# Mask products of two early batches behind a score seed, and half of the value block copies on GpSimd

## The chip, the cores and the metric

The kernel runs on one core of a Trainium2 chip. The metric is the device time of one execution in microseconds (us). The time before is the median of three runs, 596.37 us; the profile is one further execution.

## What is computed

The reference is a graph attention layer on 16 batches of 512 nodes with 512 features, in float32. It adds two directions of attention (d = 0, 1); each node attends with 16 heads of width 32 to the first 20 nodes of its batch. Cut to what matters:

```python
q_exp = where(row_zero, 0, q)                       # row_zero: the node's features sum to 0
self_feat = concat([v, q_exp]) @ W_self.T + b_self  # 512 nodes x 512
output = self_feat
for d in range(2):
    A = (adj if d == 0 else swap(adj))[:, :, :20, :]  # 11 integer labels for each pair of nodes
    cond, vb = A.sum(-1), A @ w_bias + b_bias
    qh, kh = heads(self_feat @ Wq[d].T + bq[d]), heads(self_feat[:, :20] @ Wk[d].T + bk[d])
    aff = where(cond > 0, qh @ kh / sqrt(32), -9e15) + vb
    output += heads_out(softmax(aff) @ self_feat[:, :20], Wout[d]) + bout[d]
return v + relu(output)
```

## The kernel before

**Setup.** The first 100 us or so load the weights and form, for all batches at once, the keys (written to the DRAM tensors `g1_d`, for batch 1, and `g_d`, for the later ones; batch 0's stay in `g0`) and the values (`vw_d`). The values are also needed as small 32x32 blocks with zeros around them: `clear_blocks` fills the DRAM tensor `bd_d` with zeros, and twelve DRAM-to-DRAM copies, `fill_block` 0 to 11 (L185, steps `bl00` to `bl11`), put pieces of 128 bytes from `vw_d` into it. Each copies 64 x r pieces, with r rows from 4 to 20. All batches' blocks are filled by these twelve copies, so the load of batch 0's blocks (`load_values`, step `Lvd`, tile `vd`, four loads a batch) waits for all of them.

**Loop.** After that the work is a list of small steps, each recorded on one engine. `ORDER` (L17) is a table of step names with an offset: in turn t the step `mul3+1` is done for batch t+1. The turns run from -1 to 17, and the code walks through the table once per turn (L1131); a step is left out where `first` (L1108) says that it has no work for that batch. Each engine executes its own steps strictly in this order. Loads are DMAs issued by the sync engine's queue (SP), also in order; `behind` ties a load to an instruction recorded five steps earlier, so that loads don't run ahead. Each DMA also waits until the DMA eight places ahead of it on its queue has landed.

In turn t, TensorE (PE) does three things for 512 nodes: seven score products S1 to S7 of batch t (L440; a fast 2x2 block scheme, accumulated in the PSUM tiles `ps_a` and `ps_d`), the attention sum O of the batch before (L550, which reads `vd`), and seven feature products F1 to F7 of batch t+1 (L292, into four banks `ps_o`). The order on PE is S1, S2, S6, O, S7, S5, F1, S4, F6, S3, F7, F5, F2, F4, F3. Around them stand, by batch t:

- S1 adds to `ps_a`; step `t11` (`take`, L487, ScalarE = ACT) copies it to the softmax tile `s_11`; S6 then adds on to `ps_a`, so it can't start before that copy.
- S2 adds to `ps_d`; `f11` (`join`, L496, VectorE = DVE) adds it to `s_11`. Then `sc` (`seed`, L482, ACT) puts a new start value into `ps_d` for S5.
- `t12` (L492, DVE) takes `ps_a` after S6, and S7 waits for it.
- `mx11` (L503, DVE), `sub11` (L507, GpSimd = POOL), `exp11` (L511, ACT), `sum11` (L515, DVE) and so on are the softmax of `s_11`.
- `z`, `y` and `t` tiles (L409, L421, L267, POOL) are the operand sums of the block schemes.
- `p1` (L337, ACT) copies bank 0 after F1, and F6 reuses the bank.

The masks of batch t+1 are made in turn t too: `load_adj` brings the tile `adj` (a single buffer, two loads), eleven steps `mul0` to `mul10` (`mask_mul`, L363, ACT) multiply one label each by its weight into `prod`, `cnt` (`mask_count`, L369, DVE) sums the labels, `flg` (L375, L376, ACT) turns the sum into a flag, and `msum` (L381, DVE) adds `prod` up. In the table most of the `mul` steps stand ahead of `t11` and `sc`.

Of the kernel before, what the change touches and what calls it, by code (L numbers as in the profile page):

```python
# [17 lines left out]
Z3+0 Z2+0 mul1+1 S2+0 mul2+1 Lx2+1 LG3+1 rec12-1 n22b-2 mul0+1 turn22-1 rb3-2 m22a-1 mul7+1 fu22+0  # L18
turn21-1 bl06+0 nor12-1 bl00+0 bl05+0 t11+0 S6+0 rb1-2 f11+0 bl02+0 P1+0 Lx3+1 Y3+0 u22a-1 turn12-1 e11+0
t12+0 mul9+1 bl09+0 mul10+1 bl11+0 so2-1 mul3+1 P4b-1 mul4+1 Lxn1+2 x22a-1 O0-1 Oa-1 mul6+1 O1-1 Lnz+1  # L20
k1+0 Z1+0 mul8+1 Lxn3+2 S7+0 Y4+0 mul5+1 sc+0 rb2-2 m22b-1 mx11+0 Ladj0+2 kv+1 oe2-1 flg+1 Lvd0+0 k2+0
oe3-1 rs0+2 S5+0 X1+1 sub11+0 LG1+1 oe0-1 F1+1 exp11+0 u22b-1 LG2+1 Lcq+2 ra0-2 v22a-2 rs2+2 t22+0 oe1-1
s22a-1 S4+0 bl01+1 msum+1 rs1+2 Z4+0 bl07+1 sum11+0 LG0+2 f22+0 Lx0+2 v22b-2 bl08+1 sA1-2 rs3+2 mx22+0
X2+1 f21+0 x22b-1 rm+2 p1+1 sp1+1 rec11+0 rb0-2 Ob-2 F6+1 bl04+1 bl10+1 nq+1 rst+2 P3+0 st1-1 ra3-1 bl03+1
nc+1 ra1-1 X3+1 Lxn0+3 sp0+1 S3+0 p2+1 P2+0 Ladj1+2 e21+0 mx21+0 sub22+0 exp22+0 Lvd3+0 nor11+0 nd+1 Oc-2
sub21+0 F7+1 rc0-2 exp21+0 X4+1 Lvd2+0 k3b+0 Lvd1+0 r22a-1 Lxn2+3 f12+0 F5+1 e12+0 sum22+0 p3+1 n22a-1
F2+1 F4+1 sd+1 st3-1 sA0-2 mx12+0 rec22+0 sum21+0 j3+1 sub12+0 rc2-2 nr+1 k0+1 st2-1 rec21+0 k3a+0 F3+1
# [8 lines left out]
def gat_kernel(  # L36
# [20 lines left out]
    nc = tc.nc  # L57
    B, F, N = xT.shape
# [112 lines left out]
    def blocks():  # L171

        bb = bd_d.rearrange("c b r e i g -> (c b) r e i g")
        vv = vw_d.rearrange("d c (b m) (e g) -> d (c b) m e g", m=NG, e=HL)
        for e in range(HL):
            for i in range(2):
                j = (e * S) // 32 + i
                for d in range(2):
                    lo = max(e * S + d * NG, 32 * j)
                    hi = min(e * S + (d + 1) * NG, 32 * j + 32)  # L180
                    if lo < hi:
                        m, r = lo - e * S - d * NG, lo - 32 * j
                        yield bb[:, r : r + hi - lo, e, i], vv[d, :, m : m + hi - lo, e]

    def fill_block(n):  # L185
        to, of = list(blocks())[n]
        nc.sync.dma_start(to, of)

    def ran(ins):
        done["all"].append(ins)  # L190
# [847 lines left out]
    with tc.manual_schedule():  # L1038
# [19 lines left out]
        for n in range(len(list(blocks()))):  # L1058
            steps[f"bl{n:02d}"] = lambda b, n=n: fill_block(n)
# [67 lines left out]
        NOT_END |= {f"{x}22" for x in ("mx", "sub", "exp", "sum", "rec", "nor", "turn")} | {"sa", "sd", "sc", "O0", "O1"}  # L1127
        NOT_END |= {f"{x}{ij}" for x in "tf" for ij in (11, 12, 21, 22)} | {f"{x}{c}" for x in ("oe", "st") for c in range(C)}
        order = [(w[:-2], int(w[-2:])) for w in ORDER.split()]
        fresh = True  # L1130
        turns = [(name, turn_ + ahead) for turn_ in range(-1, B + 2) for name, ahead in order]  # L1131
        for name, b in turns:
            if b in first(name):
                if fresh and (name in ("S6", "nd", "nc") or name[0] == "F" or name[:2] == "so"):
                    fresh = False
# [57 lines left out]
```

## Time and profile before

| what | value |
|---|---|
| runs | 594.38, 596.37, 598.05 us (median 596.37) |
| profiled execution | 591.75 us, its span 590.0 us |
| PE busy | 560.5 us, 95% of the span, 13980 matmuls |
| DVE, ACT, POOL busy | 433.7, 413.4, 427.8 us |
| DMA queue of SP (q1) | 123.73 MB; GpSimd's (q0) 1.36 MB |
| granted TensorE clock | 0.987 over the span |

Busy is the time in which an engine executes something. Since PE is busy for 95% of the span, the question of any change is whether it takes away some of the 29 us in which PE is idle, or adds to them. In the table of forty slices the first slices, up to about 145 us, are where PE, DVE, ACT and POOL are visibly emptier than later.

### The profile page before, as it was taken

Reading aid. Unit: us, or ns where it says so; the run is one execution under the profiler, and the core shown is the slowest. Engines: PE = TensorE matmul, PEld = TensorE weight load, DVE = VectorE, ACT = ScalarE, POOL = GpSimd, SP = SyncE. Lnnn points to the kernel's source line nnn. Section 1 sums busy time; section 2 is a strip of 40 time slices with the busy share of each in tenths; the row PEclk is TensorE's granted clock in tenths of the full one; section 3 lists DMA queues with packets and bytes.
Section 4 is the critical chain, followed back from the end, with each engine's and each line's share of the span. In section 5 each row is a group of like instructions: output and inputs, shape, how many; then the busy total and the mean of one; then the engine's idle time right before and its main releaser. Section 6 shows DMA issues by size and latency. Waiting matters only on the chain.

```text
span 590.0 us, 31439 instructions
## 1 busy us (share of the span) xinstructions
PE 560.5 (95%) x13980; PEld 437.4 (74%) x13980; DVE 433.7 (74%) x628; ACT 413.4 (70%) x890; POOL 427.8 (73%) x374
## 2 busy tenths in 40 slices
PE   8999999697999999998999999999999999999994
PEld 5443356586878787887888888877887777899983
DVE  0576571575878787877888787878787878788765
ACT  1344571786787878786878787878786868786622
POOL 2637945476687878786888887878787878888643
PEclk9999999898999999999999999999999999999997
DMA  8999999878766767766667776767666767652222
GB/s 292 380 396 370 322 316 373 222 180 239 190 222 180 222 192 227 199 209 159 228 196 223 195 222 192 220 172 228 188 215 183 219 185 212 202 175 87 70 93 73
DMA packets 102199, 127.88 MB, mean 217 GB/s; under 512 B 21457, under 2 KB 66545, under 8 KB 100017
## 3 DMA queue, kind: packets, MB, share of 16 engines
q1 hardware_dynamic: 100272, 123.73, 67.5%
q8 instruction: 110, 1.80, 1.3%
q0 software_dynamic: 672, 1.36, 1.0%
q10 hardware_dynamic: 1120, 0.79, 0.4%
q14 instruction: 25, 0.20, 0.1%
HBM read 85.97 MB, written 40.24 MB: 214 GB/s over the span
## 4 chain that ended last, share of the span: by engine, by line
PE 83%; POOL 5%; DMA 4%; issue 4%; DVE 2%; SPq 1%; ACT 1%; DVEq 0%; POOLq 0%; ACTq 0%
PE ps_o L292 30%; PE ps_a L440 22%; PE ps_d L440 15%; PE ps_o L550 8%; PE ps_k L798 3%; PE ps_a L456 1%; DMA ws_q<-in_wsT 1%; DMA vw_d<-v 1%; POOL st L924 1%; POOL cq_d L861 1%; SPq L148 1%; PE ps_kv L748 1%; DMA g_d<-st 1%; PE ps_d L456 1%; DMA xn<-in_xn 1%
## 5 line engine op out<-in xcount | busy, mean ns | idle before, releaser
L507 POOL TENSOR_TENSOR s<-s,top 128x640 f32<-128x640 f32 x63 | 80.5, 1277 | 68.8 <-DVE top L503 68.8
L363 ACT ACTIVATE prod<-adj,wb_sb 128x160 f32<-128x160 int32 x165 | 84.8, 590 | 13.3 <-POOL t L267 7.9
L522 POOL TENSOR_TENSOR s<-s,sum 128x640 f32<-128x640 f32 x63 | 79.8, 1278 | 12.3 <-DVE sum L518 12.1
L440 PE MATMUL ps_a<-y,z 128*32 128x152 f32 x1920 | 74.0, 301 | 13.1 <-issue 8.2
L292 PE MATMUL ps_o<-t,ws_s 128*32 128x246 f32 x1440 | 83.7, 370 | 0.0
L440 PEld LDWEIGHTS ps_a<-y,z 128*32 128x32 f32 x1920 | 64.1, 112 | 21.7 <-issue 18.7
L440 PE MATMUL ps_d<-g,z 128*32 128x152 f32 x1920 | 71.3, 293 | 0.3 <-issue 0.3
L511 ACT ACTIVATE s<-s 128x640 f32<-128x640 f32 x63 | 46.1, 732 | 36.1 <-POOL s L507 35.7
L292 PEld LDWEIGHTS ps_o<-t,ws_s 128*32 128x32 f32 x1440 | 56.0, 110 | 16.6
L440 PEld LDWEIGHTS ps_d<-g,z 128*32 128x32 f32 x1920 | 64.8, 110 | 2.8 <-issue 1.2
L292 PE MATMUL ps_o<-x,ws_v 128*32 128x246 f32 (+1 forms) x960 | 59.4, 373 | 0.3 <-issue 0.3
L560 DVE SCALAR_TENSOR_TENSOR o<-ps_o,x 128x512 f32<-128x512 f32 x60 | 38.4, 683 | 22.9 <-ACT cond L375 9.3
L492 DVE TENSOR_TENSOR s<-ps_a,both 128x640 f32<-128x640 f32 x45 | 37.1, 825 | 23.4 <-PE ps_a L440 23.1
L550 PE MATMUL ps_o<-wt,vd 32*32 32x256 f32 (+1 forms) x2176 | 49.3, 381 | 4.5 <-issue 2.6
L503 DVE TENSOR_REDUCE top<-s 128x32 f32<-128x640 f32 x63 | 51.2, 812 | 0.6
L515 DVE TENSOR_REDUCE sum<-s 128x32 f32<-128x640 f32 x63 | 50.2, 798 | 0.3 <-ACT s L511 0.3
L529 DVE STREAM_TRANSPOSE wt<-s 128x640 f32<-128x640 f32 x63 | 49.4, 802 | 0.0
L533 ACT COPY ps_o<-sf 128x512 f32<-128x512 f32 x64 | 36.6, 587 | 17.7 <-DVE sf L335 15.5
L292 PEld LDWEIGHTS ps_o<-x,ws_v 128*32 128x32 f32 x960 | 37.3, 110 | 13.3 <-issue 0.8
L550 PEld LDWEIGHTS ps_o<-wt,vd 32*32 32x32 f32 x2176 | 30.9, 105 | 19.3 <-issue 6.8
L496 DVE TENSOR_TENSOR s<-ps_d,s 128x640 f32<-128x640 f32 x45 | 36.9, 820 | 9.8 <-PE ps_d L440 9.2
L390 ACT COPY both<-add 32x160 f32<-32x160 f32 x128 | 41.1, 321 | 1.7
(283 smaller groups left out, 1228.0 us busy)
## 6 DMA issues: line engine op xcount, KB each, us to landing
g<-g_d SPq DMA_DIRECT2D x60, 304.0 KB, 3.8
g_d<-st SPq DMA_DIRECT2D x16, 1064.0 KB, 7.3
out_T<-o SPq DMA_DIRECT2D x60, 256.0 KB, 4.0
xn<-in_xn SPq DMA_DIRECT2D x56, 256.0 KB, 3.7
x<-in_xT SPq DMA_DIRECT2D x56, 256.0 KB, 3.6
adj<-in_adj SPq DMA_DIRECT2D x32, 440.0 KB, 4.6
vd<-bd_d SPq DMA_DIRECT2D x64, 64.0 KB, 3.4
nz<-nz_d SPq DMA_DIRECT2D x14, 256.0 KB, 3.8
```

The source lines that it names most:

```text
L292: nc.tensor.matmul(to[bass.ts(a, R), i] if wide else to[bass.ts(a, R), i, :, HK:], lhs, mov, start=wide and i == 0, stop=k == 1, skip_grou ...
L363: ran(nc.scalar.activation(new_prod(b)[:, :, l], adjs[b][:, :, l], AF.Identity, scale=wb_sb[:, l : l + 1]))
L390: ran(nc.scalar.copy(adds[b][bass.ts(2 * pg + hp, R), :, 2 * t : 2 * t + 2], add[bass.ts(2 * pg + t, R)]))
L440: nc.tensor.matmul(to[bass.ts(q, R)], rows[:, k, q // 2, bass.ds((2 * t + u) * R, R)], keys[:, k, q % 2], start=False, stop=k == 1, skip_g ...
L503: ran(nc.vector.tensor_reduce(tops[b, ij], flat(soft_tile(b, ij)), AX.X, ALU.max))
L507: ran(engine.tensor_sub(s, s, tops.pop((b, ij)).unsqueeze(2).to_broadcast([P, 4 * 2 * HL, NG])))
L511: ran(nc.scalar.activation(s, s, AF.Exp))
L515: ran(nc.vector.tensor_reduce(tops[b, ij], flat(soft_tile(b, ij)), AX.X, ALU.add))
L522: ran(engine.tensor_mul(s, s, tops.pop((b, ij)).unsqueeze(2).to_broadcast([P, 4 * 2 * HL, NG])))
L529: ran(nc.vector.transpose(wts[b][:, j, i], soft_t.pop((b, ij)).rearrange("p v h m -> p (v h m)")))
L550: nc.tensor.matmul(to, vds[b][r, j, e, i], w[:, :, bass.ts(block, 32)], start=False, stop=i == 1, skip_group_check=True,)
L560: ran(nc.vector.scalar_tensor_tensor(o, banks[q].rearrange("p (j n) -> p j n", j=2), 0.0, of_out(xs[b], hp, pg), ALU.max, ALU.add))
```

## The change

It has two parts. The first holds back the steps `mul0` to `mul10` and `cnt` of batches 1 and 2: they are put behind the step `sc` of batch 0 and of batch 1. From batch 3 on the order is as before.

The second moves six of the twelve block copies (1, 3, 4, 7, 8 and 10) from SP's queue to GpSimd's, and from the end of turn -1 to a place in turn 0, behind `flg`.

```diff
+    LATER = (1, 3, 4, 7, 8, 10)
+
     def fill_block(n):
         to, of = list(blocks())[n]
-        nc.sync.dma_start(to, of)
+        (nc.gpsimd if n in LATER else nc.sync).dma_start(to, of)
...
-        fresh = True
-        turns = [(name, turn_ + ahead) for turn_ in range(-1, B + 2) for name, ahead in order]
+        fresh, turns, held_back = True, [], []
+        for turn_ in range(-1, B + 2):
+            for name, ahead in order:
+                b = turn_ + ahead
+                early = b in (1, 2) and (name[:3] == "mul" or name == "cnt") and ("sc", b - 1) not in turns
+                (held_back if early else turns).append((name, b))
+                if (name, b) in (("sc", 0), ("sc", 1)):
+                    turns, held_back = turns + held_back, []
```

In the table the six entries `bl01+1`, `bl03+1`, `bl04+1`, `bl07+1`, `bl08+1` and `bl10+1` become `+0` entries between `flg+1` and `Lvd0+0`. Line numbers grow by two behind the first edit: L363 is L365 in the changed kernel.

**ACT at the start of turn 0.** Rows of before: the mask products of batch 1 (`prod` from `adj`), `t11` (copy of `ps_a`), `sc` (copy into `ps_d`), then `kv`, the flag, a row sum and `exp11`.

```order
L363 ACTIVATE prod_1275<-adj_1104,wb_sb 128x160 x4
L487 COPY s_11_1316<-ps_a 128x640
L363 ACTIVATE prod_1275<-adj_1104,wb_sb 128x160 x7
L482 COPY ps_d<-cq_904 128x4x160
L347 COPY sf_1410<-kvn 128x16x5
L375 ACTIVATE cond_1234<-cond_1234,marks 128x160 x2
```

The same place in the changed kernel:

```order
L489 COPY s_11_1303<-ps_a 128x640
L484 COPY ps_d<-cq_904 128x4x160
L365 ACTIVATE prod_1388<-adj_1104,wb_sb 128x160 x11
L349 COPY sf_1404<-kvn 128x16x5
L377 ACTIVATE cond_1386<-cond_1386,marks 128x160 x2
```

Four products no longer stand ahead of `t11`, and none ahead of `sc`; the eleven follow in one piece. On DVE `cnt` (the row `cond<-adj`) moves from ahead of `f11` to behind `t12`. In turn 1 both engines change in the same way.

**GpSimd in turn 0.** Rows of before: operand sums `y` and `z` of batch 0, `t_1` of batch 1, then `sub11`.

```order
L404 TENSOR_TENSOR z_1_1367<-sf_909 128x512
L421 TENSOR_TENSOR y_4_1402<-g_83,y_2_1236 128x608
L267 TENSOR_TENSOR t_1_1451<-x_179 128x492
L507 TENSOR_TENSOR s_11_1316<-s_11_1316,top_11_1406 128x640
L409 TENSOR_TENSOR z_4_1516<-sf_909,z_2_1273 128x512
```

The same place in the changed kernel:

```order
L406 TENSOR_TENSOR z_1_1349<-sf_909 128x512
L423 TENSOR_TENSOR y_4_1383<-g_83,y_2_1228 128x608
L189 DMA bd_d<-vw_d 64x12x32
L189 DMA bd_d<-vw_d 64x20x32
L189 DMA bd_d<-vw_d 64x4x32 x2
L189 DMA bd_d<-vw_d 64x20x32
L189 DMA bd_d<-vw_d 64x12x32
L269 TENSOR_TENSOR t_1_1451<-x_179 128x492
L509 TENSOR_TENSOR s_11_1303<-s_11_1303,top_11_1400 128x640
```

The six copies now stand between `y_4` and `t_1`, with `sub11` behind them.

**SP ahead of the first load of blocks.** Rows of before: start terms `cq` of batch 1, the copies, two parts of batch 1's keys (`g`), the first half of batch 2's mask labels (`adj`), the first of the four `vd` loads.

```order
L148 DMA cq_1221<-cq_d 32x320 x4
L187 DMA bd_d<-vw_d 64x12x32
L187 DMA bd_d<-vw_d 64x4x32
L156 DMA g_1214<-g_d 128x4x152
L187 DMA bd_d<-vw_d 64x20x32
L187 DMA bd_d<-vw_d 64x4x32
L187 DMA bd_d<-vw_d 64x12x32
L187 DMA bd_d<-vw_d 64x20x32
L156 DMA g_1214<-g_d 128x4x152
L187 DMA bd_d<-vw_d 64x16x32
```

The same place in the changed kernel:

```order
L148 DMA cq_1221<-cq_d 32x320 x4
L156 DMA g_1214<-g_d 128x4x152 x2
L189 DMA bd_d<-vw_d 64x16x32
L189 DMA bd_d<-vw_d 64x20x32
L189 DMA bd_d<-vw_d 64x16x32
L189 DMA bd_d<-vw_d 64x8x32 x2
L189 DMA bd_d<-vw_d 64x20x32
L141 DMA adj_1402<-in_adj 128x880
L162 DMA vd_1415<-bd_d 32x2x256
```

Six of the twelve copies are gone from SP, all of them ahead of the loads of `adj` and `vd`.

More of the change, by code (lines that the diff above doesn't have):

```diff
@@ L20 @@
 t12+0 mul9+1 bl09+0 mul10+1 bl11+0 so2-1 mul3+1 P4b-1 mul4+1 Lxn1+2 x22a-1 O0-1 Oa-1 mul6+1 O1-1 Lnz+1
[L21 to L24, printed above, removed]
+k1+0 Z1+0 mul8+1 Lxn3+2 S7+0 Y4+0 mul5+1 sc+0 rb2-2 m22b-1 mx11+0 Ladj0+2 kv+1 oe2-1 flg+1 bl01+0 bl03+0
+bl04+0 bl07+0 bl08+0 bl10+0 Lvd0+0 k2+0 oe3-1 rs0+2 S5+0 X1+1 sub11+0 LG1+1 oe0-1 F1+1 exp11+0 u22b-1
+LG2+1 Lcq+2 ra0-2 v22a-2 rs2+2 t22+0 oe1-1 s22a-1 S4+0 msum+1 rs1+2 Z4+0 sum11+0 LG0+2 f22+0 Lx0+2 v22b-2
+sA1-2 rs3+2 mx22+0 X2+1 f21+0 x22b-1 rm+2 p1+1 sp1+1 rec11+0 rb0-2 Ob-2 F6+1 nq+1 rst+2 P3+0 st1-1 ra3-1
 nc+1 ra1-1 X3+1 Lxn0+3 sp0+1 S3+0 p2+1 P2+0 Ladj1+2 e21+0 mx21+0 sub22+0 exp22+0 Lvd3+0 nor11+0 nd+1 Oc-2
```

## The prediction

> **What bounds the kernel now.** I read the chain that ended last first, then its pieces in order of time, then a table by stage.
>
> ```profile
> PE 83%; POOL 5%; DMA 4%; issue 4%; DVE 2%; SPq 1%; ACT 1%; DVEq 0%; POOLq 0%; ACTq 0%
> ...
> 133.87 3.85 DMA xn<-in_xn
> 138.22 1.49 ACT prod L363 x3
> ...
> 197.36 2.07 PE ps_a L440 x64
> ...
> 226.77 2.07 PE ps_a L440 x64
> ```
>
> PE is the bound, so only time in which PE waits can be won. In the chain (start, duration, what) PE is left at 133.87 for a load and then for mask products on ACT, until about 140. The two last lines are S1 of two successive turns: an undisturbed turn lasts 226.77 - 197.36 = 29.41 us. The table by stage (start:end, length, then each engine's busy us, granted clock, DMA share) shows this hole's end and another one:
>
> ```profile
> 105.00:110.00 5.00, 2.25 (x37) 2.04 (x41) 2.81 (x2) 4.90 (x11) 0.00 (x1) 0.72 0.72 260
> ...
> 140.00:145.00 5.00, 4.58 (x104) 3.65 (x109) 3.90 (x6) 5.00 (x12) 4.88 (x4) 0.66 0.75 225
> ```
>
> The granted clock is 0.72 and 0.66 where PE resumes, so part of the price of a wait is paid behind it.
>
> The PE rows of the timeline (start, duration, what, and in brackets the idle time before it) show which products wait:
>
> ```profile
> 97.38 2.25 PE L440 MATMUL ps_a<-g,sf 128*32 128x152 f32 x64
> ...
> 101.63 1.04 PE L1019 MATMUL ps_o<-zero 128*128 128x512 bf16 x4
> 107.75 3.63 PE L440 MATMUL ps_a<-y,z 128*32 128x152 f32 x64 [5.08 <-issue]
> 112.42 2.27 PE L440 MATMUL ps_a<-y,z 128*32 128x152 f32 x64 [1.04 <-DVE s L492]
> ...
> 120.31 1.87 PE L292 MATMUL ps_o<-t,ws_s 128*32 128x246 f32 x32
> ...
> 132.35 2.28 PE L440 MATMUL ps_a<-g,sf 128*32 128x152 f32 x64
> ...
> 140.42 3.50 PE L440 MATMUL ps_a<-y,z 128*32 128x152 f32 x64 [3.73 <-ACT s L487]
> ...
> 166.90 2.25 PE L440 MATMUL ps_a<-g,sf 128*32 128x152 f32 x64
> ```
>
> S6 waits 5.08 us in turn 0 and 3.73 us in turn 1, both times though S1 has long ended, and takes about 3.6 us where S7 at 112.42 takes 2.27 for as many matmuls. The second wait is put down to `t11` (L487); the first only to "issue". ACT's rows explain both:
>
> ```profile
> 105.10 1.97 ACT L363 ACTIVATE prod<-adj,wb_sb 128x160 f32<-128x160 int32 x4 [7.93 <-POOL t L267]
> 106.98 0.67 ACT L487 COPY s<-ps_a 128x640 f32<-128x640 f32 x1
> 107.55 3.40 ACT L363 ACTIVATE prod<-adj,wb_sb 128x160 f32<-128x160 int32 x7
> 110.85 0.69 ACT L482 COPY ps_d<-cq 128x640 f32<-128x640 f32 x1
> 111.48 0.26 ACT L347 COPY sf<-kvn 128x80 f32<-128x80 f32 x1
> ...
> 114.38 0.74 ACT L511 ACTIVATE s<-s 128x640 f32<-128x640 f32 x1 [0.73 <-POOL s L507]
> ...
> 118.51 0.57 ACT L337 COPY sf<-ps_o 128x492 f32<-128x492 f32 x1 [1.55 <-PE ps_o L292]
> ...
> 137.74 1.97 ACT L363 ACTIVATE prod<-adj,wb_sb 128x160 f32<-128x160 int32 x4 [5.42 <-DMA xn<-in_xn]
> ```
>
> `t11` stands behind four mask products, and these wait for `adj`. At 105.10 the bracket names an engine that was done; DVE's `cnt` starts at the same moment and names the load (`105.09` below). `t11` ends at 106.98 + 0.67 = 107.65, and S6 starts 0.10 us later.
>
> **The change, part by part.** *First wait.* S1 ends at 97.38 + 2.25 = 99.63; with no product ahead of it, `t11` would be done by about 100.3, and S6 can follow the bank clearing at 101.63 + 1.04 = 102.67. That is 5.1 us earlier, and S6 then takes 2.27 instead of 3.63 us. PE alone would reach F6 at 102.67 + (120.31 - 107.75) - 1.36 = 113.9. What is late next is ACT: `adj` still lands at about 105.0, and F6 needs `p1` (118.51). From 105.10 to 118.51 two steps leave the path (`t11`: 107.55 - 106.98 = 0.57; `sc`: 111.48 - 110.85 = 0.63), and two idle pieces (0.73 and 1.55) close up: `p1` starts at 118.51 - 3.48 = 115.03 and F6 at about 115.7 instead of 120.31. First term: **4.6 us**, not 6.4; PE waits 1.8 us at F6. The eleven products cost nothing more than before; they are the same instructions.
>
> DVE must keep up:
>
> ```profile
> 105.09 1.99 DVE L369 TENSOR_REDUCE cond<-adj 128x160 f32<-128x1760 int32 x1 [6.79 <-DMA adj<-in_adj]
> ```
>
> `t12` follows S6 (102.67 + 2.27 = 104.9) and would end near 105.8, `cnt` 1.99 later near 107.8, and `mx11` comes next, more than four us ahead of its place before (GpSimd got its result at 113.08, below). So `cnt`, though now between `t12` and `mx11`, delays nothing that ends last.
>
> *GpSimd's six copies.* They come after `y_4`, with `t_1` and `sub11` queued behind them; `exp11` on ACT waits for `sub11`.
>
> ```profile
> 103.78 1.22 POOL L267 TENSOR_TENSOR t<-x 128x492 f32<-128x492 f32 x1
> 113.08 1.27 POOL L507 TENSOR_TENSOR s<-s,top 128x640 f32<-128x640 f32 x1 [8.07 <-DVE top L503]
> ...
> 46.72 0.99 POOL L883 DMA_DIRECT2D vw_d<-v  x1 [1.62 <-DVE v L881]
> ...
> 59.15 0.77 POOL L883 DMA_DIRECT2D vw_d<-v  x1
> ...
> 63.49 2.56 POOL L861 DMA_DIRECT2D cq_d<-c  x4 [0.29 <-POOL c L859]
> ...
> 69.81 1.31 POOL L883 DMA_DIRECT2D vw_d<-v  x2
> ```
>
> The trace has no such copy on GpSimd, but it has GpSimd DMAs of 64 pieces (0.64 us each, 63.49), 256 pieces (0.655, 69.81) and 512 pieces (0.77, 59.15): 0.64 plus 0.29 ns a piece, an estimate from these rows. Two copies each of 256, 768 and 1280 pieces give 2 x (0.66 + 0.84 + 0.99) = 5.0 us. Bounds: 6 x 0.64 = 3.8 us if the pieces cost nothing, and 4608 x 0.99 / 512 = 8.9 us if the longest row (46.72) were all pieces. I take 5.0, since two of the six shapes equal a row. They begin where `t_1` began, at 103.78, and end at 108.8, `t_1` at 110.0, `sub11` at 111.3; ACT wants it at 114.38 - 0.73 - 1.20 = 112.45. The cover is GpSimd's idle 8.07 us, and 1.1 us of it remains: from 6.1 us of copies on each further one costs one; the upper bound costs 2.8.
>
> *Second wait and the loads.* With `t11` free of the products, turn 1 can be an undisturbed turn: 166.90 - 132.35 = 34.55 against 29.41, a second term of **5.1 us** (3.73 of wait, the rest mostly the slow S6). With S1 of turn 1 at 132.35 - 4.6 = 127.75, O wants its `vd` tiles after three products, at 134.0, and ACT's products must start near 134.3, because 10.5 us lie between the first product and the end of `p1` (105.10 to 115.6) and F6 falls at 144.9. Before, these loads came later:
>
> ```profile
> 108.57 2.16 SPq L187 DMA_DIRECT2D bd_d<-vw_d  x2
> ...
> 111.44 2.81 SPq L187 DMA_DIRECT2D bd_d<-vw_d  x4
> ...
> 115.53 6.66 SPq L187 DMA_DIRECT2D bd_d<-vw_d  x6
> ...
> 124.99 0.34 SPq L162 DMA_DIRECT2D vd<-bd_d  x1
> ...
> 132.03 0.38 SPq L141 DMA_DIRECT2D adj<-in_adj  x1
> 132.50 1.32 SPq L162 DMA_DIRECT2D vd<-bd_d  x3
> ...
> DMA to landing us min/median/max: 3.0/5.2/5.4
> ```
>
> The second `adj` half is issued at 132.03, and the products wait until 137.74; the last line (the `vd` loads of this stage) puts the last `vd` at about 138.6. They must come 4.6 us earlier. SP loses the copies at 108.57 and 111.44, 2.16 + 2.81 = 5.0 us of an unbroken queue, so they land near 132.7 and 133.6, just in time.
>
> The Trainium skill, DMA: Bandwidth & Descriptors, section "Issuing engines are not separate DMA queues", says that DMAs of all issuing engines run on the same 16 engines and that issuing from several saves sequencer time alone. By that rule the 5.0 us of issue may be all that SP gains, and the data of the copies still has to be moved; no row here has both queues on this work.
>
> The bytes can get in the way. The xn loads that `rs` (L198, ahead of `exp11`) reads are then in flight:
>
> ```profile
> 99.33 3.11 SPq L135 DMA_DIRECT2D xn<-in_xn  x4
> ...
> DMA to landing us min/median/max: 9.2/9.3/9.6
> ```
>
> The first lands near 99.33 + 9.3 = 108.6, and ACT would read it in the step ahead of `exp11`, at about 111.7 if I give that step 0.7 us before 112.45: 3.1 us of slack. The six later copies on SP (88 rows of 64 pieces) took 124.99 - 115.53 = 9.5 us until all had landed, so the moved ones (72 rows) are worth at most 7.7 us; if all of that went ahead of the load, `rs` would lose 4.5 us. At the least it is nothing, or a little less than nothing, since the copies start earlier. I take 0.7 us for this and for loads that are just late.
>
> *Sum:* 4.6 + 5.1 - 0.7 = **9.0 us** less. Later turns keep their order and only move. The profiled execution is 591.75 us (span 590.0), so it would become 582.7; it lies 4.6 us under the median of the runs. On that median, 596.37, the forecast is **587.4 us**. One per cent of it, about what a measurement can tell, is 6.0 us.
>
> **The rivals.**
>
> *The loads aren't earlier.* If `adj` and `vd` keep landing at 137.7 and 138.6, O starts 4.6 us late and the gain is 4.4: 592.0. For it: the first `vd` load can't be issued until the last copy has landed, and DMA shares near 1 stand in the table. Against it: SP's queue has no gap between 108.57 and 132.03 that is not its own work or that landing.
>
> *The copies crowd out ACT's inputs.* Either xn is 4.5 us late, or the copies hold GpSimd for 8.9 us: the gain falls to about 4.5 to 6.2, some 591.
>
> *GpSimd is held by each copy* (slower). If GpSimd could not go on until a copy has landed, `t_1`, `sub11` and so `exp11`, `p1` and F6 would stand behind six landings. This decides from 6.1 + 9.0 = 15.1 us in all, 2.5 us a copy. The price, from the landings of GpSimd's small DMAs:
>
> ```profile
> DMA to landing us min/median/max: 3.9/4.4/6.4
> ```
>
> 6 x 4.4 = 26.4 us, 11.3 us slower: 607.7. Against it: four DMAs in 2.56 us at 63.49, each issued long before the one ahead had landed.
>
> A milder form of this stands in the Trainium skill, SBUF - State Buffer, section "SBUF: two separate sides": a VectorE copy in a two-port mode locks GpSimd out while it writes descriptors, 3100 ns instead of 620. As an estimate from that page, six copies would take 18.6 us, 3.5 us slower. Here the DMA at 46.72, beside a VectorE copy, took 0.99 against 0.77, and VectorE does reductions and additions from 105 to 109, not copies; so I give it little.
>
> *The first wait is another's.* The profile calls it "issue". If `t11` is not what S6 waits for, only the second term is left: 592. Against it: the 0.10 us between the two.
>
> **How the numbers follow.** Forecast 0.57, loads not earlier 0.16, crowding 0.14, GpSimd held 0.07, first wait another's 0.06. Faster by over 1% holds the forecast and a part of the crowding, 0.66; within 1% is most of the second, third and fifth case, 0.27; slower 0.07. The range runs from 585 (both terms in full, 9.7, and 1.7 of the spread of the runs) to 593 (a gain of 4.4 and 1.0 of spread) and leaves out about 0.15.
>
> **What would show it.** Right: `t11` by 101 and S6 near 102.7; F6 near 115.7 behind `p1`; six GpSimd DMAs of 0.65 to 1.0 us from 103.8; first `vd` issue near 120; S6 of turn 1 straight behind S2; S1 of turn 2 near 158. Wrong: S6 still waiting with `t11` done; GpSimd's DMAs over 1.5 us each; `rs` waiting for xn; O or the products waiting for loads at 134.

## The result, and the profile after

The changed kernel takes 589.18 us (median of four runs, 587.97 to 591.21) against 597.21 us for the kernel before beside it (594.38 to 600.05): ratio 0.988, 95% interval 0.983 to 0.992. A second measurement on other runs (589.91 against 596.00 us) gave 0.990, interval 0.985 to 0.995. So 6 to 8 us are won. My forecast on the median was 587.4 us, in a range of 585 to 593; the sum behind it was 9.0 us. The profiled executions differ by only 3.0 us, 588.76 against 591.75.

Below, "after" is the changed kernel; its lines are the earlier numbers plus 2. First its PE rows (start, duration, what, in brackets the idle time before it and what ended it), to be read beside those of before:

```profile
99.21 2.25 PE L442 MATMUL ps_a<-g,sf 128*32 128x152 f32 x64
...
104.42 0.46 PE L442 MATMUL ps_a<-y,z 128*32 128x152 f32 x7
106.07 2.13 PE L442 MATMUL ps_a<-y,z 128*32 128x152 f32 x57 [1.19 <-issue]
...
117.65 0.41 PE L294 MATMUL ps_o<-t,ws_s 128*32 128x246 f32 x3
...
129.69 0.29 PE L442 MATMUL ps_a<-g,sf 128*32 128x152 f32 x1
...
133.96 2.32 PE L442 MATMUL ps_a<-y,z 128*32 128x152 f32 x61
136.21 0.71 PE L552 MATMUL ps_o<-wt,vd 32*32 32x256 f32 x32
137.60 2.12 PE L552 MATMUL ps_o<-wt,vd 32*32 32x256 f32 x96 [0.68 <-issue]
139.66 1.23 PE L442 MATMUL ps_a<-y,z 128*32 128x152 f32 x31
143.36 1.32 PE L442 MATMUL ps_a<-y,z 128*32 128x152 f32 x33 [2.47 <-issue]
...
146.49 1.87 PE L294 MATMUL ps_o<-x,ws_v 128*32 128x256 f32 x30
148.76 0.37 PE L294 MATMUL ps_o<-x,ws_v 128*32 128x246 f32 x1 [0.40 <-issue]
...
162.99 0.33 PE L442 MATMUL ps_a<-g,sf 128*32 128x152 f32 x3
```

S1 of turn 0 stands 1.83 us later than in before (99.21 against 97.38), in setup code that is the same in both, so only distances between rows are compared. Both old waits ahead of S6 are gone: S6 of turn 1 runs on from S2, and S6 of turn 0 comes at 104.42, as soon as the banks are cleared. Turn 0, from S1 to S1, fell from 34.97 to 30.48 us. Turn 1 fell only from 34.55 to 33.30, where 29.41 was forecast. New in these two turns are breaks in the middle of products, put down to "issue": S6 after 7 matmuls, O after 32 of 128, S7 after 31 of 64. Nothing in the program divides a product at these places, and in before O and S7 of turn 1 ran through:

```profile
143.85 3.17 PE L550 MATMUL ps_o<-wt,vd 32*32 32x256 f32 x128
146.94 2.27 PE L440 MATMUL ps_a<-y,z 128*32 128x152 f32 x64
```

ACT's rows show what the reorder did:

```profile
101.57 0.69 ACT L489 COPY s<-ps_a 128x640 f32<-128x640 f32 x1 [2.57 <-issue]
...
107.16 5.35 ACT L365 ACTIVATE prod<-adj,wb_sb 128x160 f32<-128x160 int32 x11 [1.96 <-DMA adj<-in_adj]
...
116.95 0.55 ACT L339 COPY sf<-ps_o 128x492 f32<-128x492 f32 x1
...
132.23 0.69 ACT L489 COPY s<-ps_a 128x640 f32<-128x640 f32 x1 [2.42 <-PE ps_a L442]
...
135.81 5.38 ACT L365 ACTIVATE prod<-adj,wb_sb 128x160 f32<-128x160 int32 x11
```

`t11` (L489) is ahead of all eleven products in both turns, and the second time the products start without a wait for `adj`. The GpSimd copies and the queue of SP:

```profile
105.60 4.53 POOL L189 DMA_DIRECT2D bd_d<-vw_d  x6
...
111.75 1.28 POOL L509 TENSOR_TENSOR s<-s,top 128x640 f32<-128x640 f32 x1 [0.34 <-DVE top L505]
```

```profile
122.60 0.34 SPq L162 DMA_DIRECT2D vd<-bd_d  x1
...
129.81 0.38 SPq L141 DMA_DIRECT2D adj<-in_adj  x1
```

Six copies hold GpSimd for 4.53 us; the row by line gives shortest, median and longest in ns:

```profile
L189 POOL DMA_DIRECT2D bd_d<-vw_d x6: 647/771/901, 105.6 to 109.4; - x6
```

On SP, the first `vd` load and the second half of `adj` are issued at 122.60 and 129.81 instead of 124.99 and 132.03; less the later setup that is 4.2 and 4.1 us sooner.

### The profile page after: what moved, and what is told of

It is laid out like the page before. It is cut to its first block, busy times and chain, and to the rows that moved or that the text cites. A ratio compares the mean times of both kernels' runs of the same rounds, so it can differ in the third digit from the quotient of the medians.

```text
span 587.0 us, 31440 instructions
## 1 busy us (share of the span) xinstructions
PE 559.7 (95%) x13980; PEld 438.8 (75%) x13980; DVE 434.5 (74%) x628; ACT 413.4 (70%) x890; POOL 432.1 (74%) x380
## 4 chain that ended last, share of the span: by engine, by line
PE 86%; DMA 3%; issue 3%; POOL 2%; ACT 2%; DVE 1%; SPq 1%; DVEq 0%; ACTq 0%; POOLq 0%
PE ps_o L294 30%; PE ps_a L442 22%; PE ps_d L442 16%; PE ps_o L552 8%; PE ps_k L800 3%; DMA g_d<-st 2%; DMA ws_q<-in_wsT 1%; PE ps_a L458 1%; PE ps_v L877 1%; POOL st L926 1%; PE ps_kv L750 1%; PE ps_d L458 1%; ACT st L917 1%; PE ps_sf L232 1%; ACT sf L325 0%
## 5 line engine op out<-in xcount | busy, mean ns | idle before, releaser
L365 ACT ACTIVATE prod<-adj,wb_sb 128x160 f32<-128x160 int32 x165 | 84.5, 593 | 2.0 <-DMA adj<-in_adj 2.0
L294 PE MATMUL ps_o<-t,ws_s 128*32 128x246 f32 x1440 | 85.2, 370 | 0.0
L442 PE MATMUL ps_a<-y,z 128*32 128x152 f32 x1920 | 72.4, 294 | 8.0 <-issue 7.0
L442 PEld LDWEIGHTS ps_a<-y,z 128*32 128x32 f32 x1920 | 62.6, 110 | 16.6 <-issue 13.3
L442 PE MATMUL ps_d<-g,z 128*32 128x152 f32 x1920 | 72.7, 293 | 0.9 <-issue 0.9
L513 ACT ACTIVATE s<-s 128x640 f32<-128x640 f32 x63 | 46.0, 731 | 34.1 <-POOL s L509 33.7
L294 PEld LDWEIGHTS ps_o<-t,ws_s 128*32 128x32 f32 x1440 | 58.0, 110 | 15.2
L294 PE MATMUL ps_o<-x,ws_v 128*32 128x246 f32 (+1 forms) x960 | 60.8, 373 | 0.4 <-issue 0.4
L294 PEld LDWEIGHTS ps_o<-x,ws_v 128*32 128x32 f32 x960 | 38.9, 110 | 12.4 <-issue 1.1
```

Of the source, the lines that this page charges most:

```text
L294: nc.tensor.matmul(to[bass.ts(a, R), i] if wide else to[bass.ts(a, R), i, :, HK:], lhs, mov, start=wide and i == 0, stop=k == 1, skip_grou ...
L365: ran(nc.scalar.activation(new_prod(b)[:, :, l], adjs[b][:, :, l], AF.Identity, scale=wb_sb[:, l : l + 1]))
L442: nc.tensor.matmul(to[bass.ts(q, R)], rows[:, k, q // 2, bass.ds((2 * t + u) * R, R)], keys[:, k, q % 2], start=False, stop=k == 1, skip_g ...
L513: ran(nc.scalar.activation(s, s, AF.Exp))
```

## The experiments

In all of them "fetch" is the theory that the breaks in the trace of after suggest: the waits called issue are PE waiting for its own instructions.

**The reorder alone.** The table and the copies as before, with the rule that holds the steps back.

```diff
-    LATER = (1, 3, 4, 7, 8, 10)
+    LATER = ()          # and ORDER of the kernel before
```

> The reorder alone: the mask products and counts of batches 1 and 2 stand behind sc, all twelve copies stay on SP at their old places. Two terms (my prediction's): the first wait goes (about 4.6 us), but adj's second half and the vd tiles of turn 1 still land near 137.7 and 138.5, so O waits from about 134 to 138.6 and the second term is lost: 4 to 5 us faster than before, O the product that waits. Rival (fetch): PE cannot run turn 1 without a pause, since its instructions then come too late (the waits called issue in the kernel after, 3.5 us in turn 1); a wait at O costs little because those waits vanish beside it: 5 to 8 us faster, and no wait called issue of over 1 us in the 10 us behind O.

Measured: 592.9 us, ratio 0.997 (0.993 to 1.000), 2.1 us won, just at the edge of what can be told from nothing.

```profile
139.22 3.82 PE L552 MATMUL ps_o<-wt,vd 32*32 32x256 f32 x126 [1.42 <-DMA vd<-bd_d]
...
145.31 1.32 PE L442 MATMUL ps_a<-y,z 128*32 128x152 f32 x33 [0.67 <-issue]
```

O waits for `vd`, as the first theory said, and the break in S7 is 0.67 us instead of 2.47, as the second said. Both put the gain too high.

**The copies alone.** After, with nothing held back.

```diff
-                early = b in (1, 2) and (name[:3] == "mul" ...
+                early = b in () and (name[:3] == "mul" ...
```

> The six copies on GpSimd at their new place, the order of products as before. Two terms: the first wait stays as it was (S6 of turn 0 5 us late behind four products). In turn 1 adj's second half lands near 133 to 135, about when S1 ends at 134.6, so that the four products and t11 are late by 0 to 2 us instead of 3.7: 2 to 4 us faster than before. Rival (each half needs the other): t11 behind the products waits all the same, 0 to 1 us faster.

Measured: 594.31 us, ratio 0.996 (0.992 to 1.000), 2.7 us won. The profiled execution, 600.24 us, was the longest of its runs; only its first turns are read.

```profile
138.53 2.28 PE L442 MATMUL ps_a<-y,z 128*32 128x152 f32 x64
```

The 2.7 us lie in the 2 to 4 of the two terms. With `t11` still behind four products, S6 of turn 1 (138.53) has no wait: earlier loads remove the second wait without the reorder as long as turn 0 keeps its own. Turn 1 takes 31.94 us.

**Only batch 1, only batch 2 held back.**

```diff
-                early = b in (1, 2) and
+                early = b in (1,) and        # the other kernel: b in (2,)
```

> As after, but only batch 1 is held back; the products of batch 2 stand ahead of t11 again. Two terms: S6 of turn 0 is early, S1 of turn 1 near 128 to 129; adj lands near 135, t11 of turn 1 stands behind four products and S6 waits about 3.5 us for it: 4 to 5 us faster than before, 4 to 5 slower than after. Rival (fetch): the wait at S6 lets the instructions come in, the stall of 2.5 us in S7 of turn 1 is gone, and the kernel is no more than 2 us slower than after.

> As after, but only batch 2 is held back; turn 0 keeps the products ahead of t11. Two terms: S6 of turn 0 waits 5 us as before, turn 1 runs without the wait of 3.7 us and without the slow S6: 5 us faster than before. Rival (fetch): turn 1 meets the stall in S7 as after does, at the same matmul (31 of 64 done), so only 1 to 2 us are won.

Measured: batch 1 alone 591.36 us, ratio 0.990 (0.986 to 0.994), 6.0 us won; batch 2 alone 593.35, ratio 0.996 (0.992 to 0.999), 2.6 us won, no more than the copies alone. With batch 1 alone:

```profile
137.48 2.27 PE L442 MATMUL ps_a<-y,z 128*32 128x152 f32 x64 [3.36 <-ACT s L489]
...
144.23 1.32 PE L442 MATMUL ps_a<-y,z 128*32 128x152 f32 x33 [0.63 <-issue]
```

S6 of turn 1 waits 3.36 us again, and still the kernel is only 1.5 to 2.2 us behind the two medians of after (the intervals overlap): with the wait at S6, the break in S7 is 0.63 us (2.47 and 1.10 in the two traces of after). With batch 2 alone the break in S7 is there at the same matmul, 1.61 us long. Here the rival (fetch) came nearer both times.

**After once more, and its PE instructions shifted.** The second kernel has 16 more of the matmuls that warm PE up in the setup.

```diff
-            for _ in range(7):
+            for _ in range(7 + 16):
                 nc.tensor.matmul(warm[:, :P], ones, ones, start=True, stop=True)
```

> The kernel after once more, beside more runs of the kernel before. My forecast, on the median, is 9.0 us faster (ratio 0.985); the two profiled executions differ by 3.0 us. Theory (fetch): the waits called issue stand at the same matmuls as in the first trace of after (S6 of turn 0 after 7, O of turn 1 after 32, S7 of turn 1 after 31, O of turn 2 after 121 matmuls), all whole multiples of 256 PE instructions apart, but have other lengths, and turn 1 (S1 to S1) is 28.8 us plus their sum. Rival: they stand elsewhere from execution to execution.

> 16 matmuls are added to those that warm PE up in the setup: 32 PE instructions more ahead of everything. Theory (PE's instructions come in blocks of 256 and are late at the block's edge): every wait called issue stands 16 matmuls earlier: in S7 of turn 1 after 15 matmuls instead of 31 (49 follow), in O of turn 1 after 16 instead of 32, in O of turn 2 with 23 left instead of 7. Rival (a resource that the product itself needs, a bank or its operands): they stay at 31, 32 and 7. The time changes by less than 3 us.

Measured: 589.91 us and 593.34 us (ratio 0.996, 0.993 to 0.999). The shifted kernel is 3.4 us slower than after, where under 3 was expected; its setup is longer, with S1 of turn 0 at 101.37 us against 97.64 and 99.21 in the two traces of after. The trace of after once more:

```profile
105.19 3.39 PE L442 MATMUL ps_a<-y,z 128*32 128x152 f32 x57 [1.88 <-issue]
...
137.50 2.12 PE L552 MATMUL ps_o<-wt,vd 32*32 32x256 f32 x96 [0.91 <-issue]
...
141.89 1.32 PE L442 MATMUL ps_a<-y,z 128*32 128x152 f32 x33 [1.10 <-issue]
...
147.56 0.37 PE L294 MATMUL ps_o<-x,ws_v 128*32 128x246 f32 x1 [0.67 <-issue]
```

The same matmuls, other lengths. And the shifted kernel, whose first row counts 46 warming matmuls where after has 14 (each `matmul` of this shape is recorded as two):

```profile
1.05 7.76 PE L707 MATMUL ps_warm<-ones 128*128 128x128 f32 x46 [1.05 <-DVE ones L691]
...
138.20 2.84 PE L552 MATMUL ps_o<-wt,vd 32*32 32x256 f32 x128 [0.71 <-issue]
143.80 2.27 PE L442 MATMUL ps_a<-y,z 128*32 128x152 f32 x64 [2.76 <-POOL z L411]
...
148.35 0.32 PE L442 MATMUL ps_d<-g,z 128*32 128x152 f32 x1 [0.22 <-issue]
```

The breaks of turn 1 stand 64 PE instructions earlier, which is what was added, 32 matmuls with their loads (my 16 forgot the doubling): ahead of O's first matmul instead of its 33rd, ahead of S7's first instead of its 32nd, and ahead of S5's last. The break in S6 of turn 0 is missing: its place now falls in S2, and PE runs through it. So the breaks belong to a place in PE's instruction stream, not to a product, a bank or an operand. (The name in brackets at 143.80 is the last event the profile finds; in after S7 was half done before that `z` was begun.) The distance fits: in after, 96 + 31 = 127 matmuls lie between the break in O and that in S7, and 33 + 64 + 30 = 127 between S7 and F1; each has a weight load, and with the semaphore instructions among them each distance is 256 instructions. In all fourteen traces of this case, every gap of over 0.6 us between the starts of PE's instructions from 97 to 558 us is either a wait for a semaphore or load that stands at a product's first matmuls, or lies a whole multiple of 256 instructions from the others (to the few records that some traces lack). The page of after has the matching transfers:

```profile
q8 instruction: 110, 1.80, 1.3%
```

110 packets in 1.80 MB are 16384 bytes each, for 28220 PE instructions in the trace, 256 to a packet. The Trainium skill, Runtime: NRT & Kernel Launch, section "Instruction fetch mechanics", says just this: engines refill their instructions in blocks of 16 KiB, 256 instructions, over a DMA queue of their own, and that the cost at a block's edge is mostly hidden. The trace agrees with the first. Hidden the cost is at 84 of the 98 edges in the loop of after, where PE lost under 0.4 us, and not at the other 14.

The packets of this queue, set beside the edges, show what ends a break. In all fourteen traces each packet between 97 and 568 us has ended at least 1.0 us before PE passes its edge, and wherever PE stood still for over 0.4 us at an edge, it went on 1.1 to 1.7 us (median 1.4) behind the packet's end. And no packet starts more than 0.6 us before PE passes the edge before its own; so in these traces PE has one block in reserve and no more. In after, PE passes the edge in O at 137.60, the next packet runs from 141.11 to 142.07, and S7 goes on at 143.36.

**Twelve copies on GpSimd, and the late copies on SP.** All twelve behind `flg`, or after's table with all copies issued by SP.

```diff
-    LATER = (1, 3, 4, 7, 8, 10)
+    LATER = tuple(range(12))     # bl00, 02, 05, 06, 09, 11 moved behind bl10;  the other kernel: ()
```

> All twelve copies on GpSimd, one behind the other where after has six: the suspected cost on GpSimd doubled. My prediction's threshold: after has 1.1 us of cover left, the six more cost 4.5 to 5.5 us there, so sub11, exp11 and p1 are 3.5 to 4.5 us later and F6 waits for p1; SP is free 5.8 us sooner, but the loads were in time already: 3 to 4 us slower than after. Rival (exp11's lateness is taken up by PE, as p1 is not what F6 waits for in after): the same as after within 1.5 us. Theory fetch adds: a wait at F6 shortens the waits called issue in turn 1, so no more than 2 to 3 us slower.

> The copies at after's place in the program, but issued by SP: all twelve stand together behind the first half of adj for batch 2. Theory: GpSimd's share is what brings the loads earlier; here SP issues as much as in before, and the second half of adj and the vd tiles of turn 1 land near 137 to 139 again, O waits 2 to 4 us for vd, and the kernel is 2 to 5 us faster than before, as with the reorder alone. Rival (the place, not the engine, counts): as fast as after.

Measured: twelve on GpSimd 590.39 us, ratio 0.991 (0.987 to 0.994); late on SP 593.07, ratio 0.997 (0.994 to 1.001). With twelve, GpSimd (L508 is `sub11`), ACT (L512 is `exp11`) and PE:

```profile
103.62 6.06 POOL L188 DMA_DIRECT2D bd_d<-vw_d  x8
110.88 3.18 POOL L188 DMA_DIRECT2D bd_d<-vw_d  x4 [1.19 <-DMA bd_d<-vw_d]
```

```profile
116.58 0.74 ACT L512 ACTIVATE s<-s 128x640 f32<-128x640 f32 x1 [4.44 <-POOL s L508]
```

```profile
119.75 3.49 PE L293 MATMUL ps_o<-t,ws_s 128*32 128x246 f32 x32 [1.97 <-ACT sf L338]
```

The threshold exists: `exp11` waits 4.44 us for GpSimd, and F6 comes 22.5 us behind S1 (97.23) instead of 18.4. Half is about as much as GpSimd has room for. But the kernel is not measurably slower than after, as the rival said, though not for its reason, since F6 does wait for `p1`. Something gives this back in the runs. Turn 1 is shorter than in both traces of after (31.77 us), which is not enough, and the profiled execution (595.76 us) lies 5.4 us above the median of its runs; this stays open. With the copies late on SP, 1.6 us are won by the ratio, not told from none, and O and even S1 wait for loads:

```profile
130.86 2.02 PE L442 MATMUL ps_a<-g,sf 128*32 128x152 f32 x56 [1.27 <-DMA g<-g_d]
...
140.06 2.82 PE L552 MATMUL ps_o<-wt,vd 32*32 32x256 f32 x126 [1.02 <-DMA vd<-bd_d]
```

So the engine counts, not the place.

**Why the instructions are late.** Less traffic (64 of 512 columns of each `xn` row loaded and summed, and 64 of 512 of each output row stored for all batches but the last), and more (two copies of 512 KB that nothing reads, in each of turns 4 to 7).

```diff
-        behind(nc.sync.dma_start(xns[b, j // 2][:, j % 2], src), ins)
+        behind(nc.sync.dma_start(xns[b, j // 2][:, j % 2, :64], src[:, :64]), ins)
...
-        t = xns[b, j // 2][:, j % 2]
+        t = xns[b, j // 2][:, j % 2, :64]
...
-        nc.sync.dma_start(out[b, bass.ts(c, P)], os[b][:, c])
+        nc.sync.dma_start(out[b, bass.ts(c, P), :64], os[b][:, c, :64])
```

```diff
...
+        if 6 <= b < 10:     # with each half of adj
+            behind(nc.sync.dma_start(more[i, b % 2], xn[b, i * (N // 2) : (i + 1) * (N // 2)]), ins)
```

> After with about a third less traffic in the later turns: of each xn row 64 of 512 columns are loaded and summed, and of each output row of all batches but the last 64 of 512 columns are stored (the rest of both is left out). PE's instructions are the same. Theory (the blocks of PE instructions are late because the DMA engines are full): the waits at the edges of blocks, 21 to 22 us in all behind 97 us in the two profiles of after, fall to 5 to 12 us, the stall in S7 of turn 1 goes below 1 us, and the kernel is 8 to 15 us faster than after. Rival (a block simply takes that long to fetch, however busy the engines): they stay at 18 to 24 us, and the time within 3 us of after.

> After with two more copies from memory to memory in each of turns 4 to 7 (512 KB each, of xn, that nothing reads), beside the two adj loads. Theory (full DMA engines): in these four turns, about 224 to 345 us, the waits called issue at the edges of blocks grow from 5 to 6 us in the profiles of after to 9 to 20 us, and they stay as they are outside: 4 to 15 us slower than after. Other loads get later as well, and where PE then waits for a load it counts for neither. Rival: only waits for loads grow, those at the edges of blocks stay within 2 us.

Measured: less traffic 579.04 us, ratio 0.974 (0.968 to 0.979), some 8 to 11 us faster than after with the same PE instructions; a part of ACT's work (the sums) went with the bytes. The waits of PE put down to issue (what, total us, times, longest), between 97 and 568 us, in after and then with less traffic:

```profile
PE ps_a L442 <- issue: 7.0, 6, 2.5
PE ps_o L552 <- issue: 2.8, 3, 1.1
PE ps_d L442 <- issue: 0.9, 3, 0.4
PE ps_o L294 <- issue: 0.4, 1, 0.4
```

```profile
PE ps_a L442 <- issue: 3.0, 3, 2.0
PE ps_o L552 <- issue: 1.5, 3, 0.6
PE ps_d L442 <- issue: 1.0, 3, 0.5
PE ps_o L294 <- issue: 0.4, 1, 0.4
```

11.1 us against 5.9. Counted at every 256th PE instruction, with the short gaps that these rows leave out (the longest step between two matmuls' starts within a few instructions of the edge, less the usual 0.03 us), it is 21.1 us (22.2 in the second trace of after) against 14.1: less, though not the 5 to 12 that I wrote. The same count at other fixed places of the blocks finds 4 to 5 us of ordinary unevenness in each of these traces, so the edges themselves cost some 16 to 18 us in after and 9 with less traffic. More traffic gave 592.13 us, ratio 0.995 (0.992 to 0.997), slower than after by 2 to 4 us; but in turns 4 to 7 these waits are 4.8 us against 3.2 and 4.7 in the two traces of after, which is no growth to speak of, where 9 to 20 us had been forecast. Traffic matters, but its amount alone doesn't set the wait. How busy the DMA engines are just then goes with it, by a comparison inside the traces: where they were over 90% busy in the 1.5 us behind an edge, the next packet began 1.9 us behind that edge in the mean of after's 24 such edges, and where they were under half busy, 0.7 us (16 edges); in all fourteen traces it is 1.6 to 2.1 against 0.4 to 0.8 us.

**The spacing of the loads.** `PACE` sets how many recorded instructions back a load is tied.

```diff
-PACE = 4
+PACE = 2     # the other kernel: 7
```

> After, with each load held behind an instruction 2 instead of 4 places back, so that fewer loads stand in the queues at once. Theory (full DMA engines): the queue ahead of a block of instructions is a little shorter, 0 to 4 us faster than after. Rival (loads become late): PE waits for g, vd or adj, 0 to 10 us slower than after.

> After, with each load held behind an instruction 7 instead of 4 places back: loads may start earlier, where their buffer is free. In the run with 2 places they stood closer together (landing 6 to 8 us behind their issue instead of 3 to 5) and the waits at the edges of blocks grew from 21 to 34 us. Theory (a block is late where many loads stand ahead of it): with 7 the loads spread out, the sum falls to 12 to 19 us, and the kernel is 2 to 8 us faster than after. Rival (4 is where the loads stand farthest apart, and with 7 they crowd somewhere else): the sum stays at 19 to 25 us, the time within 3 us of after or slower.

Measured: 605.83 us with 2 (ratio 1.018, 1.012 to 1.024) and 604.99 with 7 (ratio 1.012, 1.005 to 1.020). I had expected neither to lose so much, and by the theory a small gain from both. With 7 the same view gives:

```profile
PE ps_d L442 <- issue: 13.2, 7, 2.5
PE ps_a L442 <- issue: 7.1, 6, 2.5
PE ps_o L294 <- issue: 4.5, 3, 2.2
PE ps_o L552 <- issue: 1.1, 2, 0.9
```

25.9 us, and 23.7 with 2; counted at every 256th instruction, 35.3 and 34.1. These runs move the same bytes as after. The kernels are some 15 us slower than after in their medians and 16 to 20 in the traces, of which 12 to 14 are PE waiting for instructions; between 97 and 568 us no row has it waiting for a load. The moment at which loads are issued thus moves this kernel more than the change did. Why 4 lies so well was not found out; no version that does the whole work beat after.

## Why the prediction was right or wrong

**First wait: right, 4.6 us forecast, 4.5 in the trace** (34.97 to 30.48 us from S1 to S1; 3.1 in the second trace, where the break in S6 is 1.88 us and S6 slow behind it). Less the later setup, `t11` ends at 100.4 ("by 101"), S6 starts at 102.6 (102.67), `p1` ends at 115.67 and F6 starts at 115.8 (115.7). The 1.8 us for which PE was to wait at F6 are taken mostly by the break in S6 instead (1.19 us in its row), and so cost nothing more. That the profile's "issue" ahead of S6 was `t11` is confirmed: it went when the products moved.

**Copies on GpSimd: right.** 5.0 us forecast, 4.53 measured, 0.65 to 0.90 us each; `sub11` ends at 113.03, 111.2 less the later setup (111.3). The twelve copies show that the cover ends about where I put it. GpSimd was not held by landings, and the lock-out of the Trainium skill, SBUF - State Buffer, section "SBUF: two separate sides", didn't show: with VectorE's additions and reductions beside them no copy took over 0.90 us.

**Loads: right.** First `vd` issue at 120.8 less the later setup (about 120), no wait at O or at the products. The two kernels without that gain wait for `vd`. Of the 0.7 us for crowding nothing was seen: `rs` reads xn without a wait. (The loss put on a late xn should read 4.6 us, 7.7 - 3.1; the sum doesn't use it.) SP gained 4.1 to 4.2 us, not more than the 5.0 us of issue taken from it: the trace agrees with the rule of the Trainium skill, DMA: Bandwidth & Descriptors, section "Issuing engines are not separate DMA queues", that a second issuing engine saves sequencer time alone.

**Second term: the step that failed.** I took 5.1 us, since turn 1 was to be an undisturbed turn of 29.41 us. It takes 33.30 (32.26 in the second trace), a gain of 1.3 to 2.3 us. The breaks that rows show in turn 1 are 0.68 + 2.47 + 0.40 = 3.55 us of the 3.9 us missing. I had put fetch at nothing, and no rival named it. Before, PE stood still for 3.73 us ahead of S6, and the block behind it had time to come; the wait was cover for the fetch. Before's own trace shows it: the packet there starts 3.80 us behind PE's last edge (139.25 against 135.45), later than any packet in turn 1 of after, but PE, held at S6, reaches the next edge only at 144.38, 4.0 us after the packet has ended (140.37). Taking the wait away brought 3.55 us (2.68 in the second trace) back within 15 us, and batch 1 alone, which keeps it, is only 1.5 to 2.2 us behind after. What keeps the engines busy just there shows in after's DMA view from 138.0 to 143.5 us (40 slices, busy tenths), and in the first queue of its short stretch from 140.90 to 141.15:

```profile
DMA  9999999999999999663213500000009983985799
```

```profile
q8 instruction: 1, 0.02, 24.1%
```

All engines are full up to 140.2 us, and the block that S7 needs starts only behind that, at 141.11, when PE has stopped (140.89) and little else is left to move. PE runs through the block ahead of it quickly, from 137.60 to 140.89, since 96 of its matmuls are O's. That full engines make blocks late is borne out by the edges above and by the run with less traffic. That a fetch starts no sooner than about the edge before it, the packets show; what holds this one for the 0.9 us from 140.2 to 141.11 isn't in any row, and stays open.

**From the profile to the median.** I carried the sum over to the median as it stood. In the traces turns 0 and 1 together are 5.74 us shorter (5.37 in the second trace of after), and the two measurements of 8.0 and 6.1 us fit that. The first two profiles differ by only 3.0 us because after's setup was 1.83 us longer, and the time from S1 of turn 2 to the end 0.92 us (423.99 against 423.07). In the second trace of after these are 0.26 and 5.71 us longer than in before, so both move between executions of one kernel. The waits at the edges tell the same: 14.9 us in before by the count above, against 21.1, but the difference lies in turns 0 and 1 (about 1 against 7), where before's two waits covered them. Behind these turns it is 14 us in both, and 16 to 19 in the second trace of after and in those of the other seven kernels that move the same bytes at the same pace. So both first profiles were among the quiet ones. By how much of the 4.6 us that is why before's lay under its median can't be said from one trace.

The sum of 9.0 was too large by 1 to 3 us against the runs and by 3.3 to 3.6 against the traces, most of it in the second term. That 587.4 and 589.18 lie so close is in part luck: beside after, the kernel before had a median of 597.21 us, not 596.37, and the first measurement won the larger of the two gains.

## What to carry to other kernels

A wait ahead of a busy stretch can be the cover of something that no row names; before counting its removal in full, ask what else uses that time. Breaks in the middle of a product that recurred at equal distances in the instruction stream were instruction fetch here: count the instructions between them, set the packets of the instruction queue beside them, and look at what else the DMA engines carry there. Where a time hangs on such waits, a single profile can be off by several us, so the sum is made against more than one, and two profiles are compared stretch by stretch before their totals are.

## What was not expected of the hardware

A block of 256 instructions lasts PE only about 4.1 us here (S1's 64 matmuls take 2.07 us in the chain, and a block holds some 127), and one packet of 16384 bytes brings it, never asked for more than about a block ahead. A packet takes about 1.0 us, and PE goes on 1.4 us behind it; so, as an estimate from these three numbers, a packet that starts more than 1.7 us behind the edge before stops PE. PE waited up to 2.5 us for one in after. Over the loop this cost some 16 to 18 us of 589, and about 30 with the same bytes at another pace of the loads. It also differed between executions of one kernel, at the same instructions.
